# Moving one channel's row sum to GpSimd and rearranging the last channel's tail in a two-layer convolution kernel

## The chip, the cores and the metric

The kernel runs on one core of a Trainium2 chip. The metric is the device time of one execution in microseconds (us); less is better. Engines are called as the profile calls them: PE (TensorE, matrix products), DVE (VectorE), ACT (ScalarE), POOL (GpSimd), SP (SyncE, which issues most transfers). Each engine works through its own queue in the order in which the program was written; an instruction at the head of a queue that waits holds everything behind it.

## The reference

The input x has 4 images, 64 channels, 256 x 256 points. Two layers follow each other, and every channel is independent of the others.

```
# layer 0: a long 2-d convolution of every channel, done with FFTs
y   = irfft2(rfft2(x) * rfft2(k))[..., :256, :256]      # k[c] = outer product of hx[c], hy[c]
x   = y + x * bias[c]
# layer 1
scores = einsum('bpsd,bptd->bpst', x, x) / 16            # a Gram matrix for each image and channel
red    = sum(scores * weights[c], axis=-1, keepdims=True)
y      = x + red                                         # one number is added to each row
mean, var = over the images and all points of channel c
out    = (y - mean) * rsqrt(var + 1e-5) * gamma[c] + beta[c]
```

The kernel k is an outer product, so the 2-d convolution is two 1-d convolutions one after the other, each a product with a triangular Toeplitz matrix. The filters hx and hy come from a small network that is computed at the start.

## The kernel before

All numbers are 32-bit floats. The loop runs over the 64 channels; the four images of a channel are worked as two pairs (v = 0, 1), two images (u) sharing the 128 partitions.

For one channel PE does three things of nearly the same size, about 4.36 us each: conv_z (L210, the first convolution, in two halves m = 0, 1), conv_x0 (L233, the second) and gram (L270, the products for red, one half for each pair). The other engines follow:

- ACT copies the result of conv_z out of PSUM in two halves (copy_z, L219). conv_x0 reads both halves: in each of its accumulations the first two of four steps read the first half of z, the last two the second.
- DVE evicts conv_x0 (L240), adding x times bias. The result x0 stays in SBUF until the output.
- DVE multiplies the Gram matrices by the weights (weigh): two row parts that are summed into one column each (L290) and one part of plain products (L294). In before, the row parts come first.
- red needs a sum over all partitions. There are two ways. By GpSimd: DVE joins the two kinds of products (spread, L304), one long partition_all_reduce of 128 x 1024 sums them (all_sum, L312), ACT copies a half of the result to other partitions (pick_red, L319), and DVE adds it to x0 in two steps, one for each pair (add_red, L326), which also give the sums of y. By PE: red_by_pe multiplies the products by a matrix of ones (L341) and the column sums by the identity (L346), for one pair at a time, into PSUM, from where DVE adds it (add_red_of, L355).
- The sums of y go through a short partition_all_reduce on GpSimd (L330); ACT makes the mean of it (minus_mean, L361), then the sums of the squares (squares, L366); a short GpSimd sum follows (sum_squares, L372, tile tot), ACT takes the root of the variance (root, L378 to L382), DVE makes scale and shift with a Newton step (scale_shift, L386 to L394).
- finish (L406, or L404 on DVE) writes one of four parts of the output tile, which SP sends out (L407), 256 KB each.

The order in each queue is written out by hand (manual_schedule). In the loop, the stages of four channels are woven together: while PE convolves channel c + 1, GpSimd sums red of channel c, and DVE adds red of c - 1. In the loop's order for ACT both halves of copy_z come before pick_red, and pick_red before root. In GpSimd's order the long sum of a channel comes before the short sum of the squares of the channel before it.

The loop ends with channel 61 (C - 3). last_channels then does what is left of 59 to 63: in it c = 63, p = 62, q = 61, f = 60, e = 59. In before, red of q, p and c is made by PE (BY_PE = C - 3). The two calls of red_by_pe for q stand between the two halves of conv_z of c. For p and c mean and variance are made in a shorter way: the mean of the first pair, doubled, serves as a preliminary mean for the squares (first_mean), and drift corrects mean and variance by the sum of the second pair.

PSUM has eight banks, given out in turn (pool ps); the output tiles o have eight buffers.

Of the kernel before, what the change touches and what calls it, by code (L numbers as in the profile page):

```python
# [16 lines left out]
P = 128  # L17
# [20 lines left out]
def conv_scores_bn_kernel(  # L38
# [54 lines left out]
    ones = const.tile([P, H], F32, name="ones")  # L93
    nc.vector.memset(ones, 1.0)

    warm = const.tile([P, 1], F32, name="warm")
# [157 lines left out]

    def gram(c, v, weighed=True):

# [4 lines left out]
        for places in (  # L261
            ((0, slice(0, 3), slice(0, 5, 2)), (1, slice(1, 4), slice(2, 7, 2))),
            ((2, slice(2, 4), slice(3, 7, 3)), (3, slice(0, 4, 3), slice(0, 4, 3))),
        ):
            for i in range(4):
                for n in range(4):
                    u, h = n % 2, n // 2
                    rows = bass.ts(u, H)
                    m, t, o = places[h]
                    nc.tensor.matmul(  # L270
                        gs[u][bass.ts(h, H), o, :],
                        lhsT=xb[rows, v, i, m, :], rhs=xb[rows, v, i, t, :],
                        start=(i == 0), stop=(i == 3),
                    )
        if not weighed:
            banks.extend(gs)
            return
# [5 lines left out]

    def weigh(c, b, g):

        _, red0, _, pr, _ = st8[c]
        w = ws[c]
        for n, part in enumerate((ROW0, ROW1)):
            junk = wk.tile([P, 3, H], F32, tag="junk", name=f"junk_{c}_{b}_{n}")
            nc.vector.scalar_tensor_tensor(  # L290
                junk, g[:, part, :], 1.0 / math.sqrt(S), w[:, 3 * n : 3 * n + 3, :],
                ALU.mult, ALU.mult, accum_out=red0[:, b, n : n + 1],
            )
        nc.vector.scalar_tensor_tensor(  # L294
            pr[:, b].rearrange("p (t s) -> p t s", s=H), g[:, COL, :], 1.0 / math.sqrt(S),
            w[:, 6:10, :], ALU.mult, ALU.mult,
        )

# [34 lines left out]

    BY_PE = C - 3

    def red_by_pe(c, v):

        _, red0, _, pr, _ = st8[c]
        rp = ps.tile([P, S], F32, tag="ps", name=f"rp_{c}_{v}")
        for u in range(2):  # L340
            nc.tensor.matmul(  # L341
                rp[bass.ts(u, H)], lhsT=ones, rhs=pr[:, 2 * v + u], start=True, stop=False
            )
        for n in range(2):
            for u in range(2):
                nc.tensor.matmul(  # L346
                    rp[bass.ts(u, H), bass.ts(n, P)],
                    lhsT=red0[:, 2 * v + u, n : n + 1].to_broadcast([P, H]),
                    rhs=eye_sb, start=False, stop=(n == 1),
                )  # L350
        return rp
# [32 lines left out]

    def scale_shift(c, mom, v, r):
        nc.vector.reciprocal(r, r)  # L386

        u = sm.tile([P, 1], F32, tag="u", name=f"u_{c}")
        nc.vector.tensor_scalar(u, v, r, r, ALU.mult, ALU.mult)
        nc.vector.tensor_scalar(u, u, -3.0, r, ALU.add, ALU.mult)  # L390
        g = sm.tile([P, 1], F32, tag="g", name=f"g_{c}")
        nc.vector.tensor_scalar(g, u, gam[:, c : c + 1], None, ALU.mult)
# [5 lines left out]

    def finish(c, g, sh, v, n, vector=False):
        part = bass.ts(n, 2)  # L400
# [4 lines left out]
        else:  # L405
            nc.scalar.activation(o, y, AF.Identity, bias=sh, scale=g)  # L406
        nc.sync.dma_start(out[c, v, n], o)  # L407

    N1 = 1.0 / (B * S * S)

    def first_mean(mom):

        nc.gpsimd.partition_all_reduce(mom[:, 2:3], mom[:, 0:1], P, RED.add)
        nc.scalar.activation(mom[:, 5:6], mom[:, 2:3], AF.Identity, scale=-2.0 * N1)
# [6 lines left out]
    def drift(mom, sums):  # L421

        d = sums[:, 4:5]
        nc.vector.tensor_scalar(d, sums[:, 1:2], mom[:, 2:3], N1, ALU.subtract, ALU.mult)
        nc.vector.tensor_scalar(sums[:, 5:6], d, d, -BN_EPS, ALU.mult, ALU.add)
        nc.vector.tensor_scalar(mom[:, 5:6], mom[:, 5:6], d, None, ALU.subtract)

    def root_of_rest(c, sums):

        nc.vector.tensor_scalar(  # L430
            sums[:, 6:7], sums[:, 2:3], sums[:, 3:4], N1, ALU.add, ALU.mult
        )
        v = sums[:, 7:8]
        nc.vector.tensor_scalar(v, sums[:, 6:7], sums[:, 5:6], None, ALU.subtract)
        r = sm.tile([P, 1], F32, tag="r", name=f"r_{c}")
        nc.scalar.activation(r, v, AF.Sqrt)
        return v, r

    def last_channels(c):
# [6 lines left out]
        copy_h(c)  # L446
        finish(*fins[e - 1], 0, 1)
        conv_x0(p, zs.pop(p))
        load_w(c)
        minus_mean(moms[f])  # L450
        squares(f, moms[f], 0)
        finish(*fins[e - 1], 1, 0)
        squares(f, moms[f], 1)
        tot = sum_squares(f, moms[f])
        fins[e] = (e, *scale_shift(e, moms[e], *scales[e]))
        begin_z(c)
        copy_z(c, 0, conv_z(c, 0))
        finish(*fins[e - 1], 1, 1)
        mom_q = sm.tile([P, 8], F32, tag="mom", name=f"mom_{q}")
        rps = [red_by_pe(q, v) for v in range(2)]  # L460
        for v in range(2):
            add_red_of(q, v, rps[v], mom_q)
        nc.gpsimd.partition_all_reduce(mom_q[:, 2:4], mom_q[:, 0:2], P, RED.add)
        scales[f] = root(f, tot)
        copy_z(c, 1, conv_z(c, 1))
        finish(*fins[e], 0, 0)
        finish(*fins[e], 0, 1)
        fins[f] = (f, *scale_shift(f, moms[f], *scales[f]))
        gram(p, 0)


        begin(c)
        minus_mean(mom_q)
        squares(q, mom_q, 0)
        squares(q, mom_q, 1)
        tot = sum_squares(q, mom_q)
        z = zs.pop(c)
        conv_x0(c, z, [0])
        mom_p = sm.tile([P, 8], F32, tag="mom", name=f"mom_{p}")
        add_red_of(p, 0, red_by_pe(p, 0), mom_p)  # L480
        conv_x0(c, z, [1])
        finish(*fins[e], 1, 0)
        finish(*fins[e], 1, 1)
        scales[q] = root(q, tot)
        fins[q] = (q, *scale_shift(q, mom_q, *scales[q]))
        finish(*fins[f], 0, 0)
        finish(*fins[f], 0, 1)
        first_mean(mom_p)
        squares(p, mom_p, 0)
        gram(p, 1)  # L490
        finish(*fins[f], 1, 0)
        finish(*fins[f], 1, 1)
        for n in range(2):
            finish(*fins[q], 0, n)
        gram(c, 0, weighed=False)
# [3 lines left out]
        add_red_of(p, 1, rp, mom_p)  # L499
        sums_p = sum_second(p, mom_p)  # L500
        squares(p, mom_p, 1)
        nc.gpsimd.partition_all_reduce(sums_p[:, 2:4], mom_p[:, 6:8], P, RED.add)
        for n in range(2):
            finish(*fins[q], 1, n)
        gram(c, 1, weighed=False)
        mom = sm.tile([P, 8], F32, tag="mom", name=f"mom_{c}")
        add_red_of(c, 0, red_by_pe(c, 0), mom)
        first_mean(mom)
        for u in range(2):
            weigh(c, 2 + u, banks.pop(0))  # L510
        rp = red_by_pe(c, 1)
        drift(mom_p, sums_p)
        scales[p] = root_of_rest(p, sums_p)
        add_red_of(c, 1, rp, mom)
        sums = sum_second(c, mom)
        squares(c, mom, 0)
        squares(c, mom, 1)
        nc.gpsimd.partition_all_reduce(sums[:, 2:4], mom[:, 6:8], P, RED.add)
        fins[p] = (p, *scale_shift(p, mom_p, *scales[p]))
        drift(mom, sums)  # L520
        finish(*fins[p], 0, 0)
        finish(*fins[p], 0, 1, vector=True)
        scales[c] = root_of_rest(c, sums)
        finish(*fins[p], 1, 0)
        finish(*fins[p], 1, 1)
        fins[c] = (c, *scale_shift(c, mom, *scales[c]))
        for v in range(2):
            finish(*fins[c], v, 0)
            finish(*fins[c], v, 1, vector=True)

# [13 lines left out]

    moms, scales, fins = {}, {}, {}
    for c in range(C - 2):
        p, q, f, e = c - 1, c - 2, c - 3, c - 4
        begin(c)
        copy_h(c + 1)
        if e >= 0:  # L550
            finish(*fins[e], 0, 1)
        if c + 2 < C and c:
# [3 lines left out]
        if q >= 0:  # L556
            minus_mean(moms[q])
            squares(q, moms[q], 0)
        if e >= 0:
            finish(*fins[e], 1, 0)  # L560
        if c + 3 < C:
# [8 lines left out]
        copy_z(c + 1, 0, conv_z(c + 1, 0))  # L570
        if e >= 0:
            finish(*fins.pop(e), 1, 1)
        load_h(c + 2, 2)
# [5 lines left out]
        if p >= 0:  # L579
            pick_red(p)  # L580
        if f >= 0:
            finish(*fins[f], 0, 0)
        if c + 3 < C:
            load_xt(c + 3, 0, 1)
        if q >= 0:
            scales[q] = root(q, tot)
        gram(c, 0)
        if p >= 0:
# [74 lines left out]
```

## Time and profile before

| | us |
|---|---|
| median of three runs (881.2 to 885.52) | 883.17 |
| the profiled execution, whole | 879.23 |
| its span, first to last instruction | 877.3 |

The profile is that of one execution, and the durations used below are its own. It lists busy time of each engine, then groups of instructions by line and tile, the waits, and a timeline of instructions with start and duration; a bracket behind a row says how long its engine had been idle and what released it. The granted clock of PE is given as a share of full speed; its mean over the span is 0.992. PE is busy 857.4 us, DVE 754.9, ACT 620.6, POOL 425.1. The groups that matter at the end:

| line, engine | what | mean ns of one |
|---|---|---|
| L312 POOL | long sum of red, 128 x 1024 | 6122 |
| L326 DVE | addition of red, 128 x 1024 | 1220 |
| L240 DVE | eviction of conv_x0, 128 x 512 | 741 |
| L366 ACT | squares, 128 x 1024 | 1143 |
| L406 ACT | output part, 128 x 512 | 811 |
| L219 ACT | copy of z, 128 x 512 | 575 |

### The profile page before, as it was taken

Reading aid. Unit: us, or ns where it says so; the run is one execution under the profiler, and the core shown is the slowest. Engines: PE = TensorE matmul, PEld = TensorE weight load, DVE = VectorE, ACT = ScalarE, POOL = GpSimd, SP = SyncE. Lnnn points to the kernel's source line nnn. Section 1 sums busy time; section 2 is a strip of 40 time slices with the busy share of each in tenths; the row PEclk is TensorE's granted clock in tenths of the full one; section 3 lists DMA queues with packets and bytes.
Section 4 is the critical chain, followed back from the end, with each engine's and each line's share of the span. In section 5 each row is a group of like instructions: output and inputs, shape, how many; then the busy total and the mean of one; then the engine's idle time right before and its main releaser. Section 6 shows DMA issues by size and latency. Waiting matters only on the chain.

```text
span 877.3 us, 55962 instructions
## 1 busy us (share of the span) xinstructions
PE 857.4 (98%) x24678; PEld 836.7 (95%) x24678; DVE 754.9 (86%) x2642; ACT 620.6 (71%) x1212; POOL 425.1 (48%) x195
## 2 busy tenths in 40 slices
PE   7999999999999999999999999999999999999993
PEld 5999999999999999999999999999999999999992
DVE  3578988988988898898898898898898898898885
ACT  2256767867777777777777777776776777776784
POOL 0236446446546546545545545645645645645600
PEclk9999999999999999999999999999999999999996
DMA  6623556565565655555555556555555555556534
GB/s 187 214 84 133 199 197 207 198 208 196 200 205 196 205 203 199 199 202 204 195 200 203 200 202 206 198 202 201 197 205 197 198 200 205 204 192 213 177 138 169
DMA packets 89914, 169.69 MB, mean 193 GB/s; under 512 B 10566, under 2 KB 11784, under 8 KB 89672
## 3 DMA queue, kind: packets, MB, share of 16 engines
q1 hardware_dynamic: 89116, 165.51, 54.8%
q8 instruction: 194, 3.18, 1.5%
q10 hardware_dynamic: 556, 0.61, 0.2%
q14 instruction: 48, 0.39, 0.1%
HBM read 98.18 MB, written 67.76 MB: 189 GB/s over the span
## 4 chain that ended last, share of the span: by engine, by line
PE 97%; DVE 1%; DMA 1%; ACT 0%; issue 0%; ACTq 0%; DVEq 0%
PE p L210 32%; PE g L270 32%; PE p L233 32%; PE rp L341 1%; PE rp L346 0%; DMA toep<-g_sb 0%; PE ph L131 0%; DVE x L355 0%; ACT o L406 0%; DMA fw_sb<-in_fw 0%; DVE fa L134 0%; DVE fa L139 0%; ACT z L219 0%; ACT fh L141 0%; DVE fk L138 0%
## 5 line engine op out<-in xcount | busy, mean ns | idle before, releaser
L312 POOL PARTITION_ALL_REDUCE rd<-sp x61 | 373.5, 6122 | 183.5 <-DVE sp L304 183.5
L233 PE MATMUL p<-toep,z 64*64 64x256 f32 (+3 forms) x8192 | 301.8, 296 | 0.1
L210 PE MATMUL p<-toep,xt 64*64 64x256 f32 (+3 forms) x8192 | 301.7, 296 | 0.1
L270 PE MATMUL g<-x 64*64 64x192 f32 (+1 forms) x8192 | 300.4, 296 | 0.1
L233 PEld LDWEIGHTS p<-toep,z 64*64 64x64 f32 x8192 | 292.5, 133 | 7.2 <-ACT z L219 0.6
L210 PEld LDWEIGHTS p<-toep,xt 64*64 64x64 f32 x8192 | 289.4, 133 | 7.4 <-PE idle L167 0.7
L270 PEld LDWEIGHTS g<-x 64*64 64x64 f32 x8192 | 287.6, 133 | 0.7 <-issue 0.4
L290 DVE SCALAR_TENSOR_TENSOR junk<-g,w 128x192 f32<-128x192 f32 x512 | 161.2, 352 | 82.7 <-PE g L270 82.7
L406 ACT ACTIVATE o<-x,sh,g 128x512 f32<-128x512 f32 x253 | 204.2, 811 | 3.1
L240 DVE SCALAR_TENSOR_TENSOR x<-xt,chan_sb,p 128x512 f32<-128x512 f32 x256 | 174.0, 741 | 8.1 <-PE p L233 8.1
L219 ACT COPY z<-p 128x512 f32<-128x512 f32 x256 | 134.4, 575 | 24.7 <-PE p L210 24.7
L366 ACT ACTIVATE sq<-x,mom 128x1024 f32<-128x1024 f32 x128 | 146.3, 1143 | 5.3 <-DVE x L355 2.0
L326 DVE SCALAR_TENSOR_TENSOR x<-x,rd 128x1024 f32<-128x1024 f32 x122 | 144.2, 1220 | 0.1
L304 DVE SCALAR_TENSOR_TENSOR sp<-eye_sb,red,pr 128x128 f32<-128x128 f32 x488 | 138.0, 345 | 0.0
L330 POOL PARTITION_ALL_REDUCE mom<-mom x61 | 24.3, 399 | 230.5 <-DVE x L326 226.4
L319 ACT COPY rd<-rd 64x512 f32<-64x512 f32 x61 | 37.5, 615 | 135.9 <-POOL rd L312 135.9
L294 DVE SCALAR_TENSOR_TENSOR pr<-g,w 128x256 f32<-128x256 f32 x256 | 107.6, 420 | 0.0
L192 ACT COPY toep<-toep 64x512 f32<-64x512 f32 x63 | 38.9, 617 | 33.1 <-DMA toep<-g_dram 24.2
L361 ACT ACTIVATE mom<-mom 128x1 f32<-128x1 f32 x62 | 18.2, 293 | 35.3 <-POOL mom L330 35.0
L290 DVE DVE_READ_ACCUMULATOR junk<-g,w 128x1 f32 x512 | 42.7, 83 | 0.0
L372 POOL PARTITION_ALL_REDUCE tot<-mom x62 | 29.7, 480 | 9.4 <-ACT sq L366 9.4
L366 ACT ACTIVATION_READ_ACCUMULATOR sq<-x,mom 128x1 f32 x128 | 23.9, 187 | 0.0
(60 smaller groups left out, 210.2 us busy)
## 6 DMA issues: line engine op xcount, KB each, us to landing
xt<-in_xT SPq DMA_DIRECT2D x256, 256.0 KB
out<-o SPq DMA_DIRECT2D x256, 256.0 KB
w<-in_wl SPq DMA_DIRECT2D x64, 320.0 KB
toep<-g_dram SPq DMA_DIRECT2D x252, 36.0 KB
g_dram<-g_sb SPq DMA_DIRECT2D x1, 320.0 KB
g_dram<-g_sb ACTq DMA_DIRECT2D x1, 320.0 KB
decay_sb<-in_decay SPq DMA_DIRECT2D x1, 256.0 KB
fw_sb<-in_fw ACTq DMA_DIRECT2D x1, 192.0 KB
```

The lines of the kernel that those rows point to most:

```text
L210: nc.tensor.matmul(p1[u][bass.ts(v, H), k, : S - H * i], lhsT=xts[c, v][rows, i, bass.ts(2 * m + k, H)], rhs=toep[rows, 1, H * i : S], sta ...
L219: nc.scalar.copy(zs[c][:, u, bass.ts(m, 2), :], p1[u][:, :, ::-1])
L233: nc.tensor.matmul(p2[v][bass.ts(u, H), i, : S - H * k], lhsT=z[rows, u, k, bass.ts(2 * m + i, H)], rhs=toep[rows, 0, H * k : S], start=(k ...
L240: nc.vector.scalar_tensor_tensor(x0[:, v, part], xt[v][:, part], chan_sb[:, 0, c : c + 1], p2[v][:, :, ::-1], ALU.mult, ALU.add,)
L270: nc.tensor.matmul(gs[u][bass.ts(h, H), o, :], lhsT=xb[rows, v, i, m, :], rhs=xb[rows, v, i, t, :], start=(i == 0), stop=(i == 3),)
L290: nc.vector.scalar_tensor_tensor(junk, g[:, part, :], 1.0 / math.sqrt(S), w[:, 3 * n : 3 * n + 3, :], ALU.mult, ALU.mult, accum_out=red0[: ...
L294: nc.vector.scalar_tensor_tensor(pr[:, b].rearrange("p (t s) -> p t s", s=H), g[:, COL, :], 1.0 / math.sqrt(S), w[:, 6:10, :], ALU.mult, A ...
L304: nc.vector.scalar_tensor_tensor(sp[:, b, part], eye_sb, red0[:, b, n : n + 1], pr[:, b, part], ALU.mult, ALU.add,)
L312: nc.gpsimd.partition_all_reduce(rd.rearrange("p b s -> p (b s)"), sp.rearrange("p b s -> p (b s)"), P, RED.add)
L326: nc.vector.scalar_tensor_tensor(x0[:, v], x0[:, v], 1.0, rd[:, 2 * v, None, :].to_broadcast([P, 4, S]), ALU.mult, ALU.add, accum_out=mom[ ...
L366: nc.scalar.activation(sq, st8[c][0][:, v], AF.Square, bias=mom[:, 5:6], accum_out=mom[:, 6 + v : 7 + v])
L406: nc.scalar.activation(o, y, AF.Identity, bias=sh, scale=g)
```

## The change

BY_PE becomes C - 2: red of q = 61 goes through spread, all_sum, pick_red and add_red like that of the channels before it, and red_by_pe is called for p and c only.

In last_channels, pick_red of q stands behind the second half of copy_z of c, add_red of q ahead of gram of p's first pair, and conv_x0 of c runs in one piece. root of f stands where it stood, between the two halves of copy_z.

Outputs are moved: the last three parts of 58 are written before copy_h of 63 (parts_of), and the first two parts of 59 ahead of copy_z of c.

For c = 63, red of the first pair is made by PE after the first quarter of the Gram products of its second pair (between). For the second pair the plain products come ahead of the row parts (rows_last=False) and red_by_pe finishes one image before it begins the next (together=False); two matmuls into an unused bank (none) stand ahead of it. The last addition and the last squares are done in two halves (last_part, last_squares), and the two sums over partitions are made by PE with a constant matrix (each, made at the start) and matmuls of one column (sum_of) in place of GpSimd. The Newton step for p stands ahead of the last addition, its scale, shift and first output (now on DVE) behind it. The very last output is issued from ACT's queue.

In root_of_rest four small steps for p go from DVE to ACT.

```
-    BY_PE = C - 3
+    BY_PE = C - 2
...
+                if between and i == 1:
+                    between()
+                    between = None
...
+    def sum_of(c, name, cols):
+        total = ps.tile([P, 1], F32, tag="ps", name=f"{name}_{c}")
+        for n, (sign, col) in enumerate(cols):
+            nc.tensor.matmul(
+                total, lhsT=each[:, sign], rhs=col, start=(n == 0), stop=(n == len(cols) - 1)
+            )
+        return total
...
         tot = sum_squares(f, moms[f])
         fins[e] = (e, *scale_shift(e, moms[e], *scales[e]))
+        for n in range(2):
+            finish(*fins[e], 0, n)
         begin_z(c)
         copy_z(c, 0, conv_z(c, 0))
-        finish(*fins[e - 1], 1, 1)
-        mom_q = sm.tile([P, 8], F32, tag="mom", name=f"mom_{q}")
-        rps = [red_by_pe(q, v) for v in range(2)]
-        for v in range(2):
-            add_red_of(q, v, rps[v], mom_q)
-        nc.gpsimd.partition_all_reduce(mom_q[:, 2:4], mom_q[:, 0:2], P, RED.add)
         scales[f] = root(f, tot)
         copy_z(c, 1, conv_z(c, 1))
-        finish(*fins[e], 0, 0)
-        finish(*fins[e], 0, 1)
+        pick_red(q)
+        for n in range(2):
+            finish(*fins[e], 1, n)
         fins[f] = (f, *scale_shift(f, moms[f], *scales[f]))
+        moms[q] = add_red(q)
         gram(p, 0)
...
-        gram(c, 1, weighed=False)
+        rps = []
+        gram(c, 1, weighed=False, between=lambda: rps.append(red_by_pe(c, 0)))
         mom = sm.tile([P, 8], F32, tag="mom", name=f"mom_{c}")
-        add_red_of(c, 0, red_by_pe(c, 0), mom)
+        add_red_of(c, 0, rps[0], mom)
+        sum_first(mom)
+        drift(mom_p, sums_p)
+        scales[p] = root_of_rest(p, mom_p, sums_p)
         first_mean(mom)
         for u in range(2):
-            weigh(c, 2 + u, banks.pop(0))
-        rp = red_by_pe(c, 1)
...
+            weigh(c, 2 + u, banks.pop(0), rows_last=False)
+        none = ps.tile([P, S], F32, tag="ps", name="none")
+        for n in range(2):
+            nc.tensor.matmul(none[:H], lhsT=ones, rhs=each, start=True, stop=True)
+        rp = red_by_pe(c, 1, together=False)
+        last = sm.tile([P, 8], F32, tag="last", name=f"last_{c}", bufs=1)
+        nc.scalar.copy(last[:, 5:6], mom[:, 5:6])
         squares(c, mom, 0)
-        squares(c, mom, 1)
...
+        u_p = newton(p, *scales[p])
+        for n in range(2):
+            last_part(c, rp, last, n)
+            last_squares(c, last, n)
+        d_c = sum_of(c, "d", [(0, mom[:, 0:1]), (1, last[:, 0:1]), (1, last[:, 1:2])])
+        s_c = sum_of(c, "s", [(1, mom[:, 6:7]), (1, last[:, 2:3]), (1, last[:, 3:4])])
+        fins[p] = (p, *scale_shift_of(p, mom_p, u_p))
+        finish(*fins[p], 0, 0, vector=True)
...
+        finish(*fins[c], 1, 1, queue=nc.scalar)
```

## Prediction

> **What bounds the kernel now.** I read the page's busy shares first, then the waits, then the timeline of the last 45 us engine by engine, then the granted clock in short windows. Channels are numbered from 0; the changed ones are 59 to 63.
>
> ```profile
> PE 857.4 (98%) x24678; PEld 836.7 (95%) x24678; DVE 754.9 (86%) x2642; ACT 620.6 (71%) x1212; POOL 425.1 (48%) x195
> ...
> PE 97%; DVE 1%; DMA 1%; ACT 0%; issue 0%; ACTq 0%; DVEq 0%
> ```
>
> PE is busy 98% of the span, so up to the last Gram matrix only PE time removed or PE time lost moves the end. The change touches nothing before channel 60's iteration but two memsets; everything is decided after 832 us. The tail of before, from the timeline: the last Gram matrix ends on PE at 859.4 (857.06 + 2.40), red of 63's second pair at 865.63, the last squares at 868.24, then one sum, the root, and the last outputs:
>
> ```profile
> 867.00 1.15 ACT L366 ACTIVATE sq<-x,mom 128x1024 f32<-128x1024 f32 x1 [1.16 <-DVE r L386]
> ...
> 868.33 0.41 POOL L518 PARTITION_ALL_REDUCE sums<-mom  x1 [0.95 <-ACT sq L366]
> ...
> 869.44 0.20 ACT L436 ACTIVATE r<-sums 128x1 f32<-128x1 f32 x1 [0.50 <-DVE sums L434]
> 869.55 2.96 ACT L406 ACTIVATE o<-x,sh,g 128x512 f32<-128x512 f32 x4
> ```
>
> Columns: start, duration, engine, line, operation. After the last compute (872.51) the transfers run at some 400 GB/s until 875.3, and 2.0 us later the span ends: eight outputs of 256 KB, about 0.65 us each, all behind 62's scale and shift.
>
> **What is removed.** Two calls of red by PE for channel 61. They stand between the two halves of 63's first convolution (conv_z): from 839.49 to 841.37, **1.9 us of PE**. Also gone at the tail: the GpSimd sum of the squares and one of the first moments.
>
> **What comes in their place.** Channel 61 now goes the way of every channel: spread on DVE, the long GpSimd sum, the copy by ACT (pick_red), the two additions. One iteration earlier these rows stand so:
>
> ```profile
> 826.00 6.12 POOL L312 PARTITION_ALL_REDUCE rd<-sp  x1 [2.42 <-DVE sp L304]
> 832.03 0.48 POOL L372 PARTITION_ALL_REDUCE tot<-mom  x1
> ...
> 839.51 0.40 POOL L372 PARTITION_ALL_REDUCE tot<-mom  x1 [3.76 <-ACT sq L366]
> ```
>
> ```profile
> 832.15 0.62 ACT L319 COPY rd<-rd 64x512 f32<-64x512 f32 x1 [2.29 <-POOL rd L312]
> ...
> 841.27 0.29 ACT L378 ACTIVATE tot<-tot 128x1 f32<-128x1 f32 x1
> ```
>
> The first two POOL rows are 60's long sum and the short sum of 59's squares right behind it; the third is the short sum of 60's squares, with no long sum ahead of it; the ACT rows are 60's pick_red, which waits 2.29 us for the long sum, and the root of 60, which waits for nothing.
>
> An iteration is 13.08 us (819.69 to 832.77 for the start of the second convolution). So 61's sum runs on GpSimd from 839.08 to 845.20, and the short sum tot of 60's squares, queued behind it, ends at about 845.6, not at 839.9 as in before. In a normal iteration nothing minds: root comes after both copies of z. In the changed order for the last channels, ACT does copy z(63) first half, **root of 60 (which waits for tot)**, copy z second half, pick_red of 61. So the root starts at 845.62; its three steps take 0.82 (833.51 to the next instruction at 834.33); the two copies of z 1.07, ending at 847.5; pick_red ends at 848.0.
>
> **What waits behind it.** PE: the first convolution ends at 841.57, the Gram matrix of 62's first pair at 843.75, and then the second convolution of 63 (conv_x0) wants z. The first half of z is late as well: ACT has two outputs of 59 ahead of it, which wait for 59's scale on DVE (829.72 + 13.08 = 842.8) and take 0.71 each, so its copy ends at about 845.3. PE stands 1.55 us, works 0.7 of 1.09 us = 0.76 us on the first half of z, and stands again from 846.05 to 847.5: **3.0 us lost where 1.9 were saved.** DVE is worse off. It waits for pick_red until 848.03, in front of everything: the additions of 61 start there instead of at 840.77.
>
> From 848.03 DVE has one queue without a gap. Start-to-start times from rows: two additions 2.29 (832.80 to 835.09); products of two banks 1.78 (855.91 to 857.69); four evictions of the second convolution 2.63 (825.75 to 828.38); one addition 1.14 (857.69 to 858.83); reciprocal and two Newton steps 0.83 (843.04 to 843.87); scale and shift 0.44 (853.70 to 854.14).
> - additions of 61: to 850.32; products of 62 first pair: 852.10; evictions of 63: 854.73; addition of 62: 855.87; Newton for 61: 856.6; products of 62 second pair: 858.4; scale and shift of 61: 858.84; products of 63 first pair: 860.62; additions of 62 and 63: 862.9; two drift steps (0.24 + 0.2): 863.3; products of 63 second pair: 865.1; Newton for 62: 865.85.
>
> Does any other engine come later? PE, from 847.5: second convolution to 850.35, red 852.15 to 853.2 (1.02, 848.07 to 849.09), two Gram halves of 2.2 to 857.65, red when the products are there, 859.5, a quarter of the last Gram matrix, red of 63 at 861.6 (wanted at 861.76), the rest of the Gram matrix at 863.15 (wanted at 863.3), two empty matmuls, last red at 865.6 (wanted at 865.85). ACT: 61's mean at 851.0, squares to 854.1, root 854.7 to 855.5 (wanted at 855.87); four outputs of 61 from 859.15 to 862.0, 62's squares to 863.3, its root to 864.57 (wanted at 865.1). All fit, by 0.1 to 0.5 us. The interleaved red of 63 buys its place: before it was after the whole Gram matrix.
>
> **The new tail.** The last addition in halves: no such row; one of 1024 elements takes 1.14, the 512-element eviction 0.66, so a half lies between 0.57 and 0.74. I take 0.63, as the eviction is the nearest row: 866.5 and 867.1. The half squares: 0.58 (z copy of 512, L219) to 0.80 (outputs, L406), plus the 0.19 read; I take 0.62, half of 1.15 and a little: they end at **868.0, against 868.24**. Sums by single-column matmuls do not occur; the nearest rows are eye columns at 0.076 a record (8 in 0.61) and 0.25 at half clock (1.48 for 6), so six records take 0.1 to 1.5; I take 0.35. They hide behind DVE, which after 867.1 does scale and shift (0.5), 62's first output (0.54), and three small steps (0.24 each), ending at 868.8. The GpSimd sum they replace had 0.41 and a hop. Root at 868.85 against 869.44; scale and shift as before 1.5 later, at 870.4; then ACT, after 62's last two outputs, does 63's last two, 0.71 + 0.80, to 871.98 against 872.51. 62's first output is ready at 868.2 against 868.94, and the eight transfers follow it back to back, so they end at 874.6 against 875.3. Issue of the last transfer from ACT's queue: 0.37 to 0.64 in the rows at the start, 0.33 to 0.41 on SP; between 0.3 lost and 0.3 gained, taken as 0. The extra outputs moved in front of copy_h(63) end it at 837.1 where PE wants it at 837.2; without that cover 0.7 at most. On SP, the load of 63's weights stands behind 58's outputs, but waits for DVE until 837.8 either way and is wanted at 858.8; 61's four transfers are over by 863. The memsets at the start (0.11 to 0.17 each) lie in DVE's 2.5 us wait for a load.
>
> **The sum.** The new path is 845.62 (tot of 60) + 2.41 (root, z, pick_red) + 17.82 (DVE's list) + 1.25 (two halves) + 1.75 (62's scale and output, three steps) = 868.85 at the root. Against before: 61's additions start +7.3; last red on PE ends 865.6 against 865.63, 0.0; last squares -0.2; root **-0.6**; end of the transfers -0.65. The 7.3 are made up because DVE, which idled 6.1 us between 840.77 and 865.67 (18.76 busy of 24.90), no longer does, and 60's scale and shift (1.3, at 843.04 in before) fall into ACT's copies. **Forecast: -0.6 us**: span 876.7, with the 1.9 us around it 878.6, against 879.23 profiled. The median of the runs lies 3.9 above the profiled time, so 883.17 - 0.6 = **882.6**.
>
> **A rule against a row.** PE's gaps invite the clock gate:
>
> ```profile
> 860.50:862.87 2.37, 0.00 (x0) 0.03 (x1) 2.26 (x8) 1.35 (x3) 0.63 (x2) 1.00 0.43 166
> 862.87:863.17 0.30, 0.30 (x2) 0.17 (x2) 0.30 (x3) 0.00 (x0) 0.00 (x0) 1.00 1.03 403
> 863.20:865.65 2.45, 2.44 (x12) 1.37 (x10) 1.21 (x8) 1.14 (x2) 0.00 (x0) 0.50 0.01 2
> ```
>
> (Window; its length; busy PE, PEld, DVE, ACT, POOL; clock.) A gap of 2.37 us halves the clock, and 2.44 us of work does not bring it back. The Trainium skill, "TensorE: Matmul & The Clock Gate", Part 1, What's actually happening, says the clock halves only after an idle window of about 3.4 us: by it the new gaps (1.55, 1.45, 1.8) cost nothing, and the trace already speaks against it. By the row a drop is likely; at 847.5 it delays the second convolution by up to 2.8 us, to 853.2, and the eviction that needs it starts at 853.4, so nothing. A later drop costs.
>
> **Rivals.** (A, slower) The clock halves in the gap at 850.35 and does not recover. The PE work from 852.15 to the last Gram matrix, 1.02 + 2.2 + 2.2 + 1.02 + 2.2 + 1.02 = 9.66, then takes 19.3: DVE waits, +8.3, 890.9. It passes the bound of 0.5% when half clock covers 5 to 6 us of that work. For: the row above. Against: the matmuls there are nearly unbroken for 5.5 us. (B) The clock halves there and comes back after a while: 2.45 us of work, the stretch of the row above, would cost as much again, less or more by where it falls, 1 to 3 us: 884.6. (C, better) ACT's wait is shorter, as GpSimd's spans are rough. pick_red by itself could end at 845.85, 2.15 earlier: 880.4, still inside 0.5%; more cannot be had, since DVE's 18 us follow the GpSimd sum. (D, it doesn't do what it says) The halves and the PE sums bring nothing. With their upper ends the squares end at 868.4, the sums at 869.9, the root stands at 870.15, +0.7: 883.9. For: PE is at half clock by then in before; against: the products stand ready earlier.
>
> **How the numbers follow.** Forecast 0.60; A 0.06; B 0.10; C 0.08; D 0.10; 0.06 for what I don't see. The three runs before spread over 4.3 us, so 0.5% (4.4 us) is about what can be told from no change. Faster by more than that: 0.04 from the forecast and scatter, 0.03 from C, 0.02 unseen = 0.09. Slower: A 0.06, B 0.01, D 0.01, unseen 0.03 = 0.11. Same: 0.80. The range 879.4 to 886.0 takes in C with part of its scatter, B, D and the bounds of the halves; A lies outside.
>
> **What would show it.** POOL's tot of 60 right behind the sum of 61 near 845.6; ACT's root of 60 idle before it, and PE idle at L236 for ACT's z, 3 us in all; DVE without gap from 848 to 867; last squares near 868.0. Wrong, if PE runs through from 843 to 850, or if the clock is 0.5 after 854.

## The result and the profile after

The changed kernel took 882.4 us (median of 14 runs, 880.08 to 885.24), the kernel before 884.0 (14 runs, 879.94 to 895.25). The ratio is 0.9993, 95% interval 0.9978 to 1.0009: no difference that can be told. The ratio is taken from the fast runs, which leaves out the one of 895.25. The prediction said 882.6; runs that scatter like this can neither confirm nor refute its 0.6 us.

The profiled execution of the changed kernel has a span of 883.4 us, 6.1 more than that of before, and this must not be read as a loss. GpSimd starts its long sum of channel 60 at 832.78 here and at 826.00 in before, and up to that point both programs do the same work on PE. From there to the end it is 50.62 us against 51.30. One and the same kernel (the first experiment below, profiled twice) had this start at 828.05 and at 831.48. So everything below is read from the **tail**: from the start of 62's second convolution on PE to the end of the span. It was 44.53 us in before (877.3 - 832.77) and **43.80** in the changed kernel (883.4 - 839.60). Two profiles of one kernel gave tails of 41.07 and 41.37, which shows how far one tail may be trusted. The two rows, before first:

```profile
832.77 4.54 PE L233 MATMUL p<-toep,z 64*64 64x256 f32 x125
...
839.60 0.38 PE L236 MATMUL p<-toep,z 64*64 64x256 f32 x1
```

Some matmul records are missing from a trace, so the first one seen of this convolution scatters by 0.25 us: in the kernels with the GpSimd route it lies 6.26 to 6.51 us ahead of 61's long sum. For these kernels the stretch from the start of **61's long sum** to the end of the span is given too; in the changed kernel it is 883.4 - 845.86 = 37.54.

The busy shares and the chain that ended last, from the page of the changed kernel:

```profile
PE 864.5 (98%) x24670; PEld 839.0 (95%) x24670; DVE 756.6 (86%) x2650; ACT 624.0 (71%) x1220; POOL 430.7 (49%) x194
...
PE 94%; DVE 3%; ACT 1%; POOL 1%; issue 1%; DMA 0%; DVEq 0%; ACTq 0%; POOLq 0%
```

PE's share of the chain fell from 97% to 94%. DVE's rose from 1% to 3%, and ACT and POOL, each under 1% or not listed in before, have 1%: the end of the program now hangs on a long sum, a copy and then DVE.

GpSimd in the timeline, 61's long sum and the short sum of 60's squares behind it:

```profile
845.86 6.12 POOL L325 PARTITION_ALL_REDUCE rd<-sp  x1 [2.43 <-DVE sp L317]
851.89 0.48 POOL L397 PARTITION_ALL_REDUCE tot<-mom  x1
```

ACT in the same stretch: the two halves of z, the first step of the root between them, pick_red of 61:

```profile
851.04 1.05 ACT L222 COPY z<-p 128x512 f32<-128x512 f32 x2
852.41 0.29 ACT L403 ACTIVATE tot<-tot 128x1 f32<-128x1 f32 x1 [0.32 <-POOL tot L397]
...
853.12 1.05 ACT L222 COPY z<-p 128x512 f32<-128x512 f32 x2
854.19 0.61 ACT L332 COPY rd<-rd 64x512 f32<-64x512 f32 x1
```

ACT stands only 0.32 us before the root, and yet the whole second half of z and pick_red are late: a short idle time says nothing of how late an instruction is, when what stands before it in the queue is late too (here two outputs that waited 2.66 us for 59's scale). PE pays:

```profile
848.44 2.34 PE L273 MATMUL g<-x 64*64 64x192 f32 x61
851.66 1.46 PE L236 MATMUL p<-toep,z 64*64 64x256 f32 x16 [0.88 <-ACT z L222]
853.74 4.31 PE L236 MATMUL p<-toep,z 64*64 64x128 f32 x112 [0.62 <-ACT z L222]
858.34 0.62 PE L354 MATMUL rp<-pr,ones 128*64 128x256 f32 x2 [0.29 <-DVE pr L296]
```

The second convolution of 63 lies between 850.78 and 858.05, 7.27 us for 4.36 us of work: 2.9 lost. The idle times in the brackets make up only half of it, since the modelled end of a matmul reaches into the wait (16 matmuls in 1.46 us). DVE, then, waits twice more, 3.48 and 0.51 us, and from there on hardly at all:

```profile
853.06 0.16 DVE L412 RECIPROCAL r<-r 128x1 f32<-128x1 f32 x1 [3.48 <-ACT r L405]
...
854.92 1.22 DVE L339 SCALAR_TENSOR_TENSOR x<-x,rd 128x1024 f32<-128x1024 f32 x1 [0.51 <-ACT rd L332]
...
868.78 1.22 DVE L380 SCALAR_TENSOR_TENSOR x<-x,rp 128x1024 f32<-128x1024 f32 x1
...
872.89 0.69 DVE L491 SCALAR_TENSOR_TENSOR x<-x,rp 128x512 f32<-128x512 f32 x1
```

No bracket stands behind the last two rows, and none behind the rows between: from 854.92 to 872.89, 17.97 us, DVE's queue sets the pace. The end, ACT:

```profile
874.53 0.72 ACT L499 ACTIVATE sq<-x,last 128x512 f32<-128x512 f32 x1
...
875.25 0.80 ACT L437 ACTIVATE o<-x,sh,g 128x512 f32<-128x512 f32 x1
876.07 0.20 ACT L475 ACTIVATE r<-v 128x1 f32<-128x1 f32 x1
876.18 2.96 ACT L437 ACTIVATE o<-x,sh,g 128x512 f32<-128x512 f32 x4
```

From the root to the end of the span it is 7.33 us, in before 7.86. The DMA share in windows of 0.05 us shows when the last byte has moved: at 881.9, and in before at 875.35. So 1.5 us lie behind the last byte, in before 1.95.

### The profile page after: what moved, and what is told of

It reads as the page before. It is cut to its first block, busy times and chain, and to the rows that moved or that the text cites. A ratio compares the mean times of both kernels' runs of the same rounds, so it can differ in the third digit from the quotient of the medians.

```text
span 883.4 us, 55963 instructions
## 1 busy us (share of the span) xinstructions
PE 864.5 (98%) x24670; PEld 839.0 (95%) x24670; DVE 756.6 (86%) x2650; ACT 624.0 (71%) x1220; POOL 430.7 (49%) x194
## 4 chain that ended last, share of the span: by engine, by line
PE 94%; DVE 3%; ACT 1%; POOL 1%; issue 1%; DMA 0%; DVEq 0%; ACTq 0%; POOLq 0%
PE p L213 31%; PE p L236 31%; PE g L273 31%; POOL rd L325 1%; DVE junk L305 1%; DVE x L339 0%; ACT o L437 0%; PE idle L170 0%; DVE pr L296 0%; PE ph L134 0%; DVE x L243 0%; ACT z L222 0%; DMA fw_sb<-in_fw 0%; DVE sp L317 0%; PE ph L150 0%
## 5 line engine op out<-in xcount | busy, mean ns | idle before, releaser
L325 POOL PARTITION_ALL_REDUCE rd<-sp x62 | 379.6, 6123 | 186.8 <-DVE sp L317 186.8
L236 PE MATMUL p<-toep,z 64*64 64x64 f32 (+3 forms) x8192 | 303.6, 297 | 2.5 <-ACT z L222 1.5
L213 PE MATMUL p<-toep,xt 64*64 64x192 f32 (+3 forms) x8192 | 302.5, 297 | 1.3 <-issue 1.0
L222 ACT COPY z<-p 128x512 f32<-128x512 f32 x256 | 134.9, 577 | 30.8 <-PE p L213 30.5
L339 DVE SCALAR_TENSOR_TENSOR x<-x,rd 128x1024 f32<-128x1024 f32 x124 | 146.6, 1220 | 0.5 <-ACT rd L332 0.5
L317 DVE SCALAR_TENSOR_TENSOR sp<-eye_sb,red,pr 128x128 f32<-128x128 f32 x496 | 140.3, 345 | 0.0
```

What stands on the lines that cost most here:

```text
L213: nc.tensor.matmul(p1[u][bass.ts(v, H), k, : S - H * i], lhsT=xts[c, v][rows, i, bass.ts(2 * m + k, H)], rhs=toep[rows, 1, H * i : S], sta ...
L222: nc.scalar.copy(zs[c][:, u, bass.ts(m, 2), :], p1[u][:, :, ::-1])
L236: nc.tensor.matmul(p2[v][bass.ts(u, H), i, : S - H * k], lhsT=z[rows, u, k, bass.ts(2 * m + i, H)], rhs=toep[rows, 0, H * k : S], start=(k ...
L317: nc.vector.scalar_tensor_tensor(sp[:, b, part], eye_sb, red0[:, b, n : n + 1], pr[:, b, part], ALU.mult, ALU.add,)
L325: nc.gpsimd.partition_all_reduce(rd.rearrange("p b s -> p (b s)"), sp.rearrange("p b s -> p (b s)"), P, RED.add)
L339: nc.vector.scalar_tensor_tensor(x0[:, v], x0[:, v], 1.0, rd[:, 2 * v, None, :].to_broadcast([P, 4, S]), ALU.mult, ALU.add, accum_out=mom[ ...
```

## The experiments

In each excerpt of an edit, `...` stands for lines left out. The theory: the GpSimd route for 61 makes ACT late with z and pick_red, DVE starts 61's additions 7 us late, and the rearranged tail makes that up. The rival: the GpSimd route is the gain, as it spares PE 1.9 us, and the tail is worth little.

**1. The tail without the GpSimd route.** The changed kernel, but 61's red by PE in the place it had in before:

```
-    BY_PE = C - 2
+    BY_PE = C - 3
...
-        pick_red(q)
...
+        moms[q] = sm.tile([P, 8], F32, tag="mom", name=f"mom_{q}")
+        rps = [red_by_pe(q, v) for v in range(2)]
+        for v in range(2):
+            add_red_of(q, v, rps[v], moms[q])
+        nc.gpsimd.partition_all_reduce(moms[q][:, 2:4], moms[q][:, 0:2], P, RED.add)
         scales[f] = root(f, tot)
```

> The changed kernel, but red of channel 61 by PE as in before, between the two halves of 63's first convolution; all else of the change kept. Measured by the tail, from the start of 62's second convolution on PE to the end of the span: 44.5 us in before, 43.8 in the changed kernel. Theory 1 (the GpSimd route makes ACT late with z and with pick_red, DVE starts 61's additions 7 us late, and the rearranged tail makes that up): PE has no gap before the last Gram matrix but the 0.3 us for 63's products, DVE's last addition starts 3 us earlier than in the changed kernel, tail 40.8. Theory 2 (the GpSimd route saves its 1.9 us of PE, and the rearranged tail is worth little): PE pays the 1.9 us again, tail 45 to 46.

Tail 41.07. PE in its timeline:

```profile
845.67 2.36 PE L273 MATMUL g<-x 64*64 64x192 f32 x64
847.85 4.54 PE L236 MATMUL p<-toep,z 64*64 64x256 f32 x128
852.33 0.65 PE L354 MATMUL rp<-pr,ones 128*64 128x256 f32 x4
```

No bracket: the second convolution starts behind the Gram matrix, runs through, and red follows at once. DVE's first addition of 61 and the first half of the last addition:

```profile
842.83 1.21 DVE L380 SCALAR_TENSOR_TENSOR x<-x,rp 128x1024 f32<-128x1024 f32 x1
...
865.23 0.69 DVE L491 SCALAR_TENSOR_TENSOR x<-x,rp 128x512 f32<-128x512 f32 x1
```

DVE's first addition of 61 starts 8.1 us after the start of 62's second convolution (842.83 - 834.73), in the changed kernel 15.3 (854.92 - 839.60). Last addition, first half, 30.5 (865.23 - 834.73) against 33.3. The theory holds, the rival falls.

The same kernel against before, in five rounds:

> The changed kernel with red of channel 61 by PE as in before, timed against before. Its single profile had a tail of 41.1 us (before 44.5, changed kernel 43.8). Theory 1 (the rearranged tail is the gain, the GpSimd route a loss): 3.4 us less than before, ratio 0.996, interval clear of 1. Theory 2 (the tails of single profiles are within the scatter of whole runs and mean nothing for the time): ratio 1.000.

879.29 us (12 runs) against 882.88 (17 runs), ratio **0.9958, interval 0.9938 to 0.9978**: faster, clear of 1. 0.42% is 3.7 us, with the interval 1.9 to 5.5, and the tails said 3.2 to 3.5. Against the changed kernel it was not timed side by side; there the tails say 2.4 to 2.7 us less.

**2. The GpSimd route without the tail.** Before, with BY_PE, pick_red and add_red as in the changed kernel and nothing else:

```
-    BY_PE = C - 3
+    BY_PE = C - 2
...
         scales[f] = root(f, tot)
         copy_z(c, 1, conv_z(c, 1))
+        pick_red(q)
...
+        mom_q = add_red(q)
         gram(p, 0)
```

> Before, with only red of channel 61 moved to GpSimd (spread, long sum, pick_red, additions in the changed kernel's places); the tail of before kept. Theory 1: 61's additions start 7 us late, DVE's queue sets the end, and the old tail does not make it up: tail 46.7, 2.2 more than before's 44.5. Theory 2 (the GpSimd route is the gain): PE saves 1.9 us, tail 42.6 to 43.

Tail 50.53, **6.0 more** than before; I expected 2.2. The sign is the theory's, the size is not. PE in its timeline, and the granted clock (the last but two of the columns; before it the length of the window and the busy times of PE, PEld, DVE, ACT and POOL):

```profile
853.66 2.13 PE L233 MATMUL p<-toep,z 64*64 64x128 f32 x48 [2.29 <-ACT z L219]
858.27 0.62 PE L341 MATMUL rp<-pr,ones 128*64 128x256 f32 x2 [2.48 <-DVE pr L294]
...
860.96 3.09 PE L233 MATMUL p<-toep,z 64*64 64x256 f32 x64
```

```profile
856.00:858.00 2.00, 0.00 (x0) 0.00 (x0) 2.00 (x9) 0.46 (x2) 0.40 (x1) 1.00 0.68 262
858.00:860.00 2.00, 1.55 (x9) 0.94 (x10) 2.00 (x8) 1.90 (x5) 0.00 (x0) 0.74 0.00 0
860.00:862.00 2.00, 2.00 (x18) 1.31 (x19) 1.25 (x2) 2.00 (x4) 0.40 (x1) 0.50 0.04 8
862.00:864.00 2.00, 2.00 (x64) 1.72 (x60) 0.30 (x2) 1.97 (x6) 0.40 (x1) 0.90 0.68 262
```

In before's order red of 62's first pair stands in the middle of 63's second convolution. It waits 2.48 us for products that are late, the second half of the convolution stands behind it, and the clock falls as well. I had left out that the change puts this convolution in one piece. So that was tried by itself:

```
-        conv_x0(c, zs.pop(c))
+        z = zs.pop(c)
+        conv_x0(c, z, [0])
         mom_p = sm.tile([P, 8], F32, tag="mom", name=f"mom_{p}")
         add_red_of(p, 0, red_by_pe(p, 0), mom_p)
+        conv_x0(c, z, [1])
         sum_first(mom_p)
```

> The changed kernel with 63's second convolution split again around red of 62's first pair, as in before. Theory 1 (PE waits for 62's products behind 61's late additions, so the order of PE decides how much of the lateness it pays): PE idles 2.4 us ahead of red of 62, the eviction of the second half comes 0.9 us late or more; tail 44.7 if the clock stays at 1.00, up to 47.8 if it falls as after the idle stretch of 2.48 us in the kernel with the GpSimd route alone. Theory 2 (that kernel's 6 us come from the old end of the tail, not from the place of this convolution): tail 43.8.

Tail 46.83, 3.0 more than the changed kernel (by 61's long sum 40.53 against 37.54, the same). Clock by windows, columns as above:

```profile
853.00:854.00 1.00, 0.62 (x2) 0.19 (x2) 1.00 (x6) 0.94 (x3) 0.00 (x0) 1.00 0.00 0
854.00:855.00 1.00, 0.86 (x10) 0.77 (x10) 1.00 (x3) 0.97 (x3) 0.00 (x0) 0.97 0.00 0
855.00:856.00 1.00, 1.00 (x11) 0.52 (x12) 0.99 (x2) 1.00 (x3) 0.00 (x0) 0.50 0.06 16
856.00:858.00 2.00, 2.00 (x37) 1.50 (x36) 0.64 (x2) 1.97 (x6) 0.80 (x2) 0.50 0.23 89
858.00:859.00 1.00, 1.00 (x32) 0.79 (x28) 0.00 (x0) 0.97 (x3) 0.00 (x0) 0.82 0.26 98
859.00:860.00 1.00, 1.00 (x39) 0.90 (x35) 0.76 (x2) 1.00 (x3) 0.00 (x0) 1.00 0.64 248
```

After a gap of 2.47 us ahead of red, PE runs at half clock from the end of 854 to about 858.4, 3.4 us. The order of PE alone, this convolution in one piece, spares the changed kernel 3.0 us, half of what the GpSimd route costs in before's order. How much of the 3.0 is the wait and how much the clock was not taken apart.

**3. ACT's order mended.** The copies of z first, then pick_red, then root and outputs; scale and shift of 60 behind 62's products:

```
         copy_z(c, 0, conv_z(c, 0))
-        scales[f] = root(f, tot)
         copy_z(c, 1, conv_z(c, 1))
         pick_red(q)
+        scales[f] = root(f, tot)
...
         moms[q] = add_red(q)
         gram(p, 0)
+        fins[f] = (f, *scale_shift(f, moms[f], *scales[f]))
```

> The changed kernel with ACT's order mended: both copies of z, then pick_red of 61, then root of 60 and the outputs of 59; scale and shift of 60 on DVE behind the products of 62's first pair. Theory 1 (root ahead of the copy of z costs): PE's 2.9 us gap at the second convolution is gone, 61's additions start 2.1 us earlier (6.1 after the start of 62's second convolution plus the long sum), but scale and shift of 60 (1.3) now lie in DVE's unbroken queue, so tail 43.0, 0.8 less. Theory 2 (the order of ACT doesn't matter, the long GpSimd sum alone sets the time): tail 43.8 as it is.

Tail 43.13, as the theory had it within 0.2. The long sum of 61 starts 36.64 us before the end, against 37.54 in the changed kernel. ACT's pick_red now waits for the long sum alone, and DVE's first addition starts behind it:

```profile
846.12 0.62 ACT L332 COPY rd<-rd 64x512 f32<-64x512 f32 x1 [2.37 <-POOL rd L325]
...
846.76 1.23 DVE L339 SCALAR_TENSOR_TENSOR x<-x,rd 128x1024 f32<-128x1024 f32 x1 [3.07 <-ACT rd L332]
```

So ACT's order (root's place and that of 59's outputs, which were moved together) costs what was said, but mending it gives back 0.7 to 0.9 only: the GpSimd route puts the additions behind a 6.1 us sum, whatever ACT does.

**4. Parts of the tail, each undone by itself in the changed kernel.**

Whole last addition and squares, with GpSimd sums in place of PE's:

```
...
-        for n in range(2):
-            last_part(c, rp, last, n)
-            last_squares(c, last, n)
+        add_red_of(c, 1, rp, mom)
+        sums = sum_second(c, mom)
+        squares(c, mom, 1)
+        nc.gpsimd.partition_all_reduce(sums[:, 2:4], mom[:, 6:8], P, RED.add)
...
```

> The changed kernel with the last addition and the last squares whole again and their sums by GpSimd; the rest of the change kept. Theory 1 (halves and PE sums are worth 0.6 us at the root): the root 0.6 to 0.9 later; the end of the span 0.3 to 0.9 later, since the transfers follow 62's first output, tail 44.1 to 44.7. Theory 2 (the tail is bound by eight transfers behind 62's first output, whatever the root does): tail 43.8, the same within 0.1.

Tail 44.76; by the start of 61's long sum 38.33 against 37.54, so 0.8 to 1.0 late, at the upper end of the theory or just above it. But only half of this stands at the root, 30.64 us after the start of 61's long sum against 30.21: 0.4 where the theory had 0.6 to 0.9. The other 0.4 lies behind the last byte of the transfers (1.9 us against 1.5), and no run shows that the sums cause it.

Red of 63's first pair behind the whole Gram matrix:

```
-        gram(c, 1, weighed=False, between=lambda: rps.append(red_by_pe(c, 0)))
+        gram(c, 1, weighed=False)
+        rps = [red_by_pe(c, 0)]
```

> The changed kernel with red of 63's first pair behind the whole last Gram matrix, as in before. Theory 1 (the interleaving is worth what DVE's second addition and all behind it gain): that addition starts 0.9 us later; tail 44.7. Theory 2 (DVE's queue has other work then, the order on PE is free): tail 43.8.

Tail 44.92, 1.1 more. DVE's second addition waits 1.26 us for PE there.

Without the two empty matmuls (the lines with `none` taken out):

> The changed kernel without the two empty matmuls into an unused bank. Theory 1 (they end before 63's products are there and only fill a wait of 0.6 us, too short for the clock to fall): tail 43.8, the same within 0.1. Theory 2 (they hold the clock): clock 0.50 in the last red, its end 0.3 to 0.5 us later, tail 44.2.

Tail 43.88; PE idles 0.53 us ahead of the last red and the clock stays at 1.00. They are worth nothing here (by 61's long sum 37.58 against 37.54).

The last output issued by SP (`queue=nc.scalar` taken out):

> The changed kernel with its very last output issued by SP like the others. Theory 1 (the transfers stand one behind the other at some 400 GB/s, so the queue that issues the last one doesn't matter; the prediction took 0, between 0.3 lost and 0.3 gained): tail 43.8, the same within 0.2. Theory 2 (SP's queue holds the last transfer back): tail 44.1 or more.

Tail 44.50; by the start of 61's long sum 38.00 against 37.54. 0.2 of the 0.46 lies ahead of the root, where the two programs are the same, and has nothing to do with the queue: the clock had fallen to 0.50 at 869.8, and the last matmul of the sum took 0.59 us where the changed kernel's, below, took 0.38.

```profile
870.14 0.59 PE L482 MATMUL s<-last,each 128*128 128x1 f32 x2 [0.32 <-ACT sq L499]
...
875.40 0.38 PE L482 MATMUL s<-last,each 128*128 128x1 f32 x2 [0.32 <-ACT sq L499]
```

The other 0.26 lies behind the root (7.59 against 7.33), and all of it behind the last byte (1.8 us against 1.5). So the rival is right, by 0.2 to 0.3: experiment 1's kernel, with ACT's queue, needs 7.40 from the root in both of its profiles. The queue is not the whole of that stretch, since the kernel with the GpSimd sums has 1.9 there with ACT's queue too.

The outputs of 58 back in their old places:

```
-        if c >= C - 4:
-            parts[4] = [(f, 0, 1)]
...
         copy_h(c)
+        finish(*fins[e - 1], 0, 1)
...
         squares(f, moms[f], 0)
+        finish(*fins[e - 1], 1, 0)
         squares(f, moms[f], 1)
+        finish(*fins[e - 1], 1, 1)
```

> The changed kernel with the last three outputs of 58 back in their old places on ACT: behind the copy of 63's Toeplitz matrix, between the squares of 60, and behind them. Theory 1 (ACT idles 2.7 us there, waiting for 59's scale, so the outputs are hidden in either place): tail 43.8, the same within 0.1. Theory 2 (outputs ahead free ACT for the copies of z): tail 44.5 to 45.9, one to three outputs of 0.71 more.

Tail 44.11 by the convolution's first record, which is uncertain as said above; by the start of 61's long sum 37.61 against 37.54, the same. ACT's wait for 59's scale shrinks from 2.66 to 1.80 us: the outputs were hidden in either place.

## Why the prediction was right

The forecast was -0.6 us; the tails differ by 0.7, and the ratio holds nothing against it and nothing for it. The path was right: the late start of 61's additions, what makes it late, and that the new tail makes it up. That the sizes came out so near is in part luck, since two errors of about half a microsecond cancelled (the halves and the transfers, below). Setting the predicted instants beside the measured ones, with 6.78 added for the later start (61's long sum: 839.08 predicted, 845.86 measured):

| | predicted + 6.78 | measured |
|---|---|---|
| root of 60 starts on ACT | 852.40 | 852.41 |
| 61's additions on DVE | 854.81 | 854.92 |
| evictions of 63 | 858.88 | 859.00 |
| addition of 63's first pair | 868.54 | 868.78 |
| last addition, first half | 872.63 | 872.89 |
| last squares end | 874.78 | 875.34 |
| root of 63 | 875.63 | 876.07 |
| end of the span | 883.48 | 883.4 |

- **The wait behind tot, PE's 3.0 us, DVE's unbroken queue**: right, 2.9 us and 17.97 us against 3.0 and 17.82. The timeline shows them, and they are gone or shorter where experiments 1 and 3 take away the route or mend ACT's order.
- **A slip**: the prediction lets the second convolution end at 850.35; 3.6 us of it are left at 847.5, so it ends at 851.1, and measured it is 858.05 - 6.78 = 851.27. The gap ahead of red of 62 is then 1.0 by my own rows, measured 0.29 and 0.18. It did no harm, because DVE came later still; but it made rival A look likelier than it was.
- **The halves**: the additions were sized right, 0.61 from start to start (872.89 to 873.50) where I took 0.63. The squares were mis-sized: a half takes 0.72 and 0.19 for the read of its sum, 0.85 from start to start (873.68 to 874.53), where I took 0.62. With DVE 0.26 late by then the last squares end 0.56 later than forecast, and the root is only 0.15 earlier than in before instead of 0.6 (43.29 us after the start of 60's long sum against 43.44).
- **The transfers** were mis-sized the other way: from the root to the end 7.33 us where before needs 7.86; I had 7.85. I let the eight transfers follow each other without a gap and end 0.7 earlier than in before. Counted from the start of 60's long sum their last byte has moved at 49.1 us, in before at 49.35: only 0.25 earlier. The other 0.45 lies behind the last byte, for which I took the same 2 us. There the issue from ACT's queue, which I took as 0, is worth 0.2 to 0.3 by experiment 4; what makes the rest isn't shown. So the root came 0.45 later than forecast and the stretch behind it was 0.5 shorter.
- **Rivals A and B** didn't happen: the clock is 1.00 up to 875.8. PE's gaps were 0.88, 0.62 and 0.29 by the records. That such a drop of the clock can happen here the split convolution shows, at 3.0 us in all with its wait, and a gap of 2.47 us. **C** would have needed ACT's order to be mended; that gave 0.7 to 0.9, not 2.15, for 60's scale and shift, 1.3, then lie in DVE's queue. **D**: the halves and the PE sums do bring 0.4 at the root beside their GpSimd form. The half clock that D feared for the sums came in two of the other profiles (the last output on SP, and one of the two of experiment 1's kernel) and cost 0.2 us.

Where the gain went: the tail by itself is worth 3.2 to 3.5 us (experiment 1), the GpSimd route by itself costs 6.0 (experiment 2); together they come out at 0.7 less, as the tail's order on PE spares part of what the route costs. In the rearranged tail the route costs 2.4 to 2.7 (43.80 against 41.07 and 41.37). The PE time saved, 1.9 us, was never on the path once DVE waited for a GpSimd sum.

On the Trainium skill's rule that was weighed ("TensorE: Matmul & The Clock Gate", Part 1, What's actually happening): the measurements side with the row. Idle stretches of 2.37, 2.47 and 2.48 us were each followed by half clock. In the kernel with the last output on SP the clock fell at 869.8 although PE had been busy for 2.70 of the 3.40 us before, with no idle stretch above 0.48. The return after 3.4 us of work in the split kernel does agree with the rule's busy window.

## What to carry to other kernels

Before moving work from the busiest engine to an idle one, ask who waits for the result and what stands behind that waiting instruction in its queue: here 1.9 us saved on PE became a 7 us late start on DVE. When two parts of a change go together, try each alone against before; a sum of nearly nothing hid a gain of 3.7 us (1.9 to 5.5). And when the front part of a program scatters more than the change is worth, measure from a common instant to the end.

## What the runs showed of the hardware

- PE's clock fell after idle stretches of 2.37 us (before, at 863.2), 2.47 us (split convolution) and 2.48 us (GpSimd route alone), but not after one of 2.29 us (GpSimd route alone, 851.37 to 853.66), and not after the 0.53 us without the empty matmuls. The length of one idle stretch doesn't decide it: with the last output on SP it fell at 869.8 behind idle stretches of 0.48 and 0.23 us, among single-column matmuls.
- When it falls isn't fixed by the program either: in the two profiles of experiment 1's kernel it fell 33.0 and 35.5 us after the start of 62's second convolution, once ahead of the last matmul and once 2 us behind it.
- It came back after 3.4 us of matmuls at half clock (split convolution, 854.94 to 858.36; GpSimd route alone, 858.97 to 862.39), and not within the 2.45 us at the end of before.
- The scatter of whole runs comes mostly from the loop, not from the tail. The two profiles of experiment 1's kernel have spans of 875.8 and 879.9 us, and 3.4 of these 4.1 us stand already at the start of 60's long sum. In the profile of the changed kernel up to 14.25 us lie between two starts of the long sum in place of 13.08, and inside one such iteration PE stood without a cause that the profile names:

```profile
446.52 0.65 PE L236 MATMUL p<-toep,z 64*64 64x192 f32 x15 [0.35 <-issue]
```

What holds PE there stays open.
